# Output layer begun inside the last chunk of the last graph layer, with its own PSUM banks and a fixed TensorE order

## The chip, the cores and the metric

The kernel runs on one core of one Trainium2 chip. Its engines have queues of their own: TensorE (PE, with weight loads listed as PEld), VectorE (DVE), ScalarE (ACT), GpSimd (POOL) and SyncE (SP), which issues most DMAs. The metric is the device time of one execution in microseconds (us); the time before is the median of four runs, 2605.83 us (2600.69 to 2610.18). The profile shows one execution.

## The reference, cut to what matters

The network has four layers on a graph of N = 2708 nodes with 256 features; each layer adds a graph part and a feed-forward part to x. The change touches the graph parts of layers 2 and 3 (one function builds both) and the feed-forward part of layer 3, which is the last thing computed:

```python
def _L3_gnn_ref(h, adj, W, a):
    Wh = h @ W
    f1 = Wh @ a1
    f2 = Wh @ a2
    e = leaky_relu(f1[:, None] + f2[None, :], negative_slope=0.2)
    e = where(adj > 0, e, NEG_INF)
    return elu(softmax(e, axis=1) @ Wh)

def _L3_ffn_ref(x, weight, bias):
    return einsum('bsi,oi->bso', x, weight) + bias

x = x + _L3_gnn_ref(_layernorm(x), adj, L3_gnn_W, L3_gnn_a)
x = x + _L3_ffn_ref(_layernorm(x)[None], L3_ffn_weight, L3_ffn_bias)[0]
```

All matrices are float32.

## The kernel before

The nodes lie in 22 tiles of 128 rows (NT = 22; the last, LAST = 21, has 20 rows). X holds all features in SBUF for the whole program.

**The graph layer.** `gat_single` (L1301) is called with the key g2 for layer 2 and g3 for layer 3. After a head that builds V (features times a factor, and a column of the factor itself), `big_p` and `ratio`, the node columns are worked off in four chunks: three of six tiles (768 columns) and one of three tiles (384 columns, tiles 18 to 20). Per chunk there are 22 steps j (L1448). In a step, `gat_pairs` lets ScalarE make e from big_p (L731) and VectorE multiply it with the mask (L732); e has three buffers. TensorE then adds e's part times V[j] to one accumulator per tile (L1463). An accumulator is 128x257 float32 in a PSUM bank of its own; the pool has eight banks, so that of a new chunk's accumulators some lie in banks that the chunk before doesn't use. The 20 columns of tile 21 are computed at the last chunk's start by `tail_sums` (L81): 22 narrow matmuls (L87) into four quarters of a bank, a copy ts to SBUF on ScalarE (L89), and a matmul with `quarter` that adds the four quarters into another bank (L91).

At a chunk's end each tile is divided by its last column (VectorE's reciprocal rd, L1469). Layer 3 has an ELU behind this: ScalarE reads the accumulator into h with the scale rd (L1477), VectorE takes min(h, 0) into g (L1479), ScalarE the exponential of g (L1480), VectorE max(h, 0) - 1 (L1481), adds g and h (L1482) and adds that to X (L1483).

**The output layer.** `linear_ffn` (L2380) comes after the graph layer. It loads weight and bias by GpSimd's queue. `ln_stats` (L112) takes mean and variance in groups of four tiles by bn_stats and bn_aggr on VectorE (L160, L161), then Sqrt on ScalarE (L163) and a reciprocal on VectorE (L167). Then each tile t is normalised into f on VectorE (`normed`, L124), transposed in two halves on TensorE (L132), copied into ft on ScalarE (L2396), multiplied with the weight on TensorE (two matmuls, L139). GpSimd adds the bias to X (L2397), VectorE adds product and X into o (L2401, three buffers), and SP's queue writes o to HBM (L2402).

**What sets the order.** A framework schedules each engine's instructions by priorities and estimated times, so that instructions of the output layer that depend only on finished tiles can be put between those of the graph layer on the same engine. `tc.issue_after` holds an instruction behind a named one. Waits between engines are put in by the framework from tiles and pools; a pool that is closed gives its memory to the next one opened, which then waits for the readers of what lay there. `Stats.newton` (L169) computes the inverse square root on VectorE in twelve small operations without ScalarE; it exists before and is used in the graph layer's head.

Of the kernel before, what the change touches and what calls it, by code (L numbers as in the profile page):

```python
# [8 lines left out]
F32 = mybir.dt.float32  # L9
# [7 lines left out]
P = 128  # L17
# [18 lines left out]
def rows(t):  # L36
    return min(P, N - t * P)


def span(t):  # L40
    return slice(t * P, t * P + rows(t))
# [7 lines left out]
def tiles_of(start, length):  # L49
    return range(start // P, (start + length + P - 1) // P)  # L50


class Net:
# [27 lines left out]
    def tail_sums(self, pool, work, et, V):  # L81

        nc = self.nc
        ps = pool.tile([P, D + 1], F32, name="acc")
        for j in range(NT):
            g = j % 4 * 32
            nc.tensor.matmul(ps[g : g + 32], et[:, j, :], V[:, j, :], start=j < 4, stop=j >= NT - 4)  # L87
        ts = work.tile([P, D + 1], F32, name="ts", bufs=1)
        nc.scalar.copy(ts, ps)  # L89
        ps = pool.tile([P, D + 1], F32, name="acc")  # L90
        nc.tensor.matmul(ps[: rows(LAST)], self.quarter[:, : rows(LAST)], ts, start=True, stop=True)  # L91
        return ps

    def value(self, v, name):
        t = self.const.tile([P, 1], F32, name=name)
# [78 lines left out]
def cosine_gnn(net, ctx, kept, x_in):  # L174
# [7 lines left out]
    with ExitStack() as ctx:  # L182
# [101 lines left out]
        for n, (i0, iw) in enumerate(chunks(512)):  # L284
            its = tiles_of(i0, iw)
            adj_rows = {i: load_rows_of(i) for i in its}
            if n + 2 < len(chunks(512)):
                columns(*chunks(512)[n + 2])
            whole = [i for i in its if i < LAST]
            acc = [pacc.tile([P, D + 1], F32, name=f"acc{k}", tag=f"acc{k}") for k in range(len(whole))]  # L290
            for j in range(NT):
                r = rows(j)
                ps = psc.tile([P, 512], F32, name="score")
                nc.tensor.matmul(ps[:r, :iw], QK[:, 0, span(j)], QK[:, 1, i0 : i0 + iw], start=True, stop=True)  # L294
                e = work.tile([P, 512], F32, name="e")
                exp = nc.scalar.activation(e[:r, :iw], ps[:r, :iw], AF.Exp)  # L296

                if j % 4 == 1 and 0 <= j // 4 - 1 < len(its):
                    i = its[j // 4 - 1]
                    with tc.issue_after(exp.ins):  # L300
                        degree(i, adj_rows[i])
                w = len(whole) * P
                nc.vector.tensor_tensor(e[:r, :w], e[:r, :w], net.mask[:r, j, i0 : i0 + w], ALU.mult)  # L303
                if w < iw:
                    nc.vector.tensor_tensor(et[:r, j, : iw - w], e[:r, w:iw], net.mask[:r, j, i0 + w :], ALU.mult)
                for k in range(len(whole)):
                    ended = nc.tensor.matmul(  # L307
                        acc[k], e[:r, k * P : (k + 1) * P], F[:r, j, :], start=j == 0, stop=j == NT - 1
                    )
            if len(whole) < len(its):  # L310
                with tc.issue_after(ended.ins):
                    acc.append(net.tail_sums(ptail, work, et, F))
            nc.vector.tensor_scalar(
                deg[:, its[0] : its[-1] + 1], total[:, its[0] : its[-1] + 1], 0.0, None, ALU.is_gt
            )
            for k, i in enumerate(its):
                r = rows(i)
                g = work.tile([P, D + 1], F32, name="g", bufs=4)
                (nc.scalar.copy if k % 2 else nc.vector.tensor_copy)(g[:r], acc[k][:r])
                s = work.tile([P, 2], F32, name="s")  # L320
                nc.vector.tensor_copy(den[:r, i : i + 1], g[:r, D : D + 1])
                nc.vector.tensor_scalar(s[:r, 0:1], g[:r, D : D + 1], 1e-30, None, ALU.max)
                nc.vector.reciprocal(s[:r, 0:1], s[:r, 0:1])
                nc.vector.scalar_tensor_tensor(s[:r, 0:1], s[:r, 0:1], 0.5, deg[:r, i : i + 1], ALU.mult, ALU.mult)
                nc.vector.tensor_scalar(s[:r, 1:2], deg[:r, i : i + 1], -0.5, 1.0, ALU.mult, ALU.add)
                nc.vector.scalar_tensor_tensor(X[:r, i, :], g[:r, :D], s[:r, 0:1], X[:r, i, :], ALU.mult, ALU.add)
                nc.vector.scalar_tensor_tensor(X[:r, i, :], F[:r, i, :D], s[:r, 1:2], X[:r, i, :], ALU.mult, ALU.add)
# [970 lines left out]
            nc.vector.tensor_scalar(self.grow, self.grow, 1.0 - SLOPE, None, ALU.mult)  # L1298


def gat_single(net, key, head, feed, elu):  # L1301

# [4 lines left out]
    with ExitStack() as ctx:  # L1309
# [118 lines left out]
            nc.vector.tensor_copy(V[one_row, LAST, :D], ps[one_row])  # L1428
            nc.vector.memset(V[one_row, LAST, D:], float(N))
        work = ctx.enter_context(tc.tile_pool(name=f"{key}work", bufs=3))  # L1430
        pacc = ctx.enter_context(tc.tile_pool(name=f"{key}acc", bufs=8, space=PSUM))
        whole = LAST * P
        nc.gpsimd.memset(et, 0.0)
        ev = et[:, :, : N - whole]
# [7 lines left out]
        for i0 in range(0, whole, W):  # L1442
            iw = min(W, whole - i0)
            its = tiles_of(i0, iw)
            acc = [pacc.tile([P, D + 1], F32, name="acc") for _ in its]
            if i0 + iw == whole:
                acc.append(net.tail_sums(pacc, work, et, V))
            for j in range(NT):  # L1448
                e = work.tile([P, W], F32, name="e")
                masked = gat_pairs(net, e, j, i0, iw, big_p, ratio[:, j : j + 1])  # L1450
                if i0 == 0 and j == 3:
                    net.looped = masked
                if bias is not None and i0 == 0 and j == 3:

                    late = small.tile([P, D], F32, name="late", bufs=1)
                    with tc.issue_after(masked.ins):
                        nc.vector.tensor_copy(late, bias)
                    for t in range(NT):
                        r = rows(t)
                        nc.gpsimd.tensor_tensor(X[:r, t, :], X[:r, t, :], late[:r], ALU.add)  # L1460
                for k, i in enumerate(its):
                    ri = rows(i)
                    nc.tensor.matmul(  # L1463
                        acc[k][:ri], e[:, k * P : k * P + ri], V[:, j, :], start=j == 0, stop=j == NT - 1
                    )
            for k, i in enumerate([*its, LAST][: len(acc)]):
                r = rows(i)
                rd = small.tile([P, 1], F32, name="rd")
# [12 lines left out]
                nc.vector.tensor_scalar(h[:r], h[:r], 0.0, -1.0, ALU.max, ALU.add)  # L1481
                nc.vector.tensor_tensor(g[:r], g[:r], h[:r], ALU.add)  # L1482
                nc.vector.tensor_tensor(X[:r, i, :], X[:r, i, :], g[:r], ALU.add)  # L1483


def decoder_ffn(net, ctx):
# [874 lines left out]
def biased_gnn(net, head, route):  # L2361
    def results(ctx):
        return route.combine(ctx.enter_context(net.tc.tile_pool(name="g2y", bufs=1)))

    gat_single(net, "g2", head, results, False)


def elu_gnn(net, kept, head, route):
    def results(ctx):
        rest = route.combine(ctx.enter_context(net.tc.tile_pool(name="g3y", bufs=1)))  # L2370
        first = next(rest)
        with net.tc.issue_after(route.read.ins):
            reload_graph(net, kept)
        yield first
        yield from rest

    gat_single(net, "g3", head, results, True)


def linear_ffn(net, out):  # L2380

    nc, tc, a, X = net.nc, net.tc, net.a, net.X
    with ExitStack() as ctx:
        big = ctx.enter_context(tc.tile_pool(name="f3big", bufs=1))
        work = ctx.enter_context(tc.tile_pool(name="f3work", bufs=3))
        psum = ctx.enter_context(tc.tile_pool(name="f3p", bufs=3, space=PSUM))
        w = net.load_weight(big, a["f3_wT"], "w")
        b = net.load_rows(big, a["f3_b"], D, "b")
        ln = net.ln_stats()
        for t in range(NT):  # L2390
            r = rows(t)
            f = work.tile([P, D], F32, name="f")
            net.normed(f, t, ln)
            ps = net.transposed(psum, f, r)
            ft = work.tile([P, 2, P], F32, name="ft")
            nc.scalar.copy(ft[:, :, :r], ps[:, :, :r])  # L2396
            nc.gpsimd.tensor_tensor(X[:r, t, :], X[:r, t, :], b[:r], ALU.add)  # L2397
            po = psum.tile([P, D], F32, name="po")
            net.matmul_k(po[:r], ft[:, :, :r], w)
            o = work.tile([P, D], F32, name="o")  # L2400
            nc.vector.tensor_tensor(o[:r], po[:r], X[:r, t, :], ALU.add)  # L2401
            nc.sync.dma_start(out[span(t), :], o[:r])  # L2402


@with_exitstack
def net_kernel(ctx, tc, a, out):
# [14 lines left out]
    with ExitStack() as mixture:  # L2421
        head, route = decoder_ffn(net, mixture)
        with ExitStack() as graph:
            net.mask = graph.enter_context(tc.tile_pool(name="mask2", bufs=1)).tile([P, NT, N], U8, name="mask2")
            elu_gnn(net, kept, head, route)
    linear_ffn(net, out)


def clear_dispatch(net, pool):
# [121 lines left out]
```

## Time and profile before

| | |
|---|---|
| median of four runs | 2605.83 us (2600.69 to 2610.18) |
| profiled execution, its own time | 2614.9 us |
| its span in the profile | 2613.0 us |
| TensorE busy in the span | 2433.3 us, 93% |
| VectorE, ScalarE, GpSimd busy | 1477.2, 1052.0, 334.4 us |
| mean granted TensorE clock | 0.963 |
| steps of chunk three of layer 3 end, last chunk's tail sums start | 2544.29 us |
| last chunk's first step starts on TensorE | 2548.16 us |
| transposes of the output layer start | 2580.18 us |
| last addition of the output layer starts | 2610.01 us |

Times in a timeline row are: start from the beginning of the span, busy time, engine, line, operation, what is written and read, shape, count; in brackets how long the engine idled before and which instruction ended that. A float32 matmul appears as two records, a transpose as one. Rows of equal instructions are merged, so a row's busy time can cover several. In a table by stretches the columns are the stretch, its length, busy time and count of PE, PEld, DVE, ACT and POOL, the granted TensorE clock (1.00 is full), the DMA share and GB/s.

### The profile page before, as it was taken

What the parts mean: (1) busy time and instruction counts of PE and PEld (TensorE: products, weight loads), DVE (VectorE), ACT (ScalarE), POOL (GpSimd) and SP (SyncE); (2) the same over time, 40 slices, a digit from 0 to 9 for tenths busy, and PEclk for the clock granted to TensorE, in tenths of its full rate; (3) what the DMA queues carried; (4) which work ended last, traced back from release to release, by engine and by line L of the source; (5) the groups of instructions that cost most, each with busy time, mean ns of one, the idle gap of its engine ahead of it and who ended that gap; (6) DMA issues with size and microseconds to landing.
All of it is one profiled execution on the core that took longest, in us unless ns stands there. A gap on an engine that the chain in (4) does not pass through costs nothing. (4 is left out here: it accounts for less than half of the span.)

```text
span 2613.0 us, 32662 instructions
## 1 busy us (share of the span) xinstructions
PE 2433.3 (93%) x11708; PEld 1582.1 (61%) x11708; DVE 1477.2 (57%) x3288; ACT 1052.0 (40%) x1692; POOL 334.4 (13%) x476
## 2 busy tenths in 40 slices
PE   6899998999999998979799989999989999969998
PEld 4666765686333334568578854444457777747886
DVE  7753437745888876333544457788742222264556
ACT  3444453214877772321434333344422222234454
POOL 1000003100000001144130011222221111110002
PEclk9999999979999999989899999999989999979999
DMA  8899611000000003764220010000241111050001
GB/s 288 284 289 314 204 55 64 1 6 1 1 1 1 1 1 91 180 182 144 88 66 1 1 31 17 19 17 17 107 147 34 33 33 33 19 205 7 1 1 43
DMA packets 106859, 197.58 MB, mean 76 GB/s; under 512 B 8862, under 2 KB 63752, under 8 KB 103860
## 3 DMA queue, kind: packets, MB, share of 16 engines
q1 hardware_dynamic: 88010, 146.82, 18.4%
q0 software_dynamic: 14880, 43.76, 5.2%
q10 hardware_dynamic: 3806, 4.85, 0.6%
q8 instruction: 99, 1.62, 0.3%
q14 instruction: 64, 0.52, 0.1%
HBM read 135.69 MB, written 59.71 MB: 75 GB/s over the span
## 5 line engine op out<-in xcount | busy, mean ns | idle before, releaser
L732 DVE SCALAR_TENSOR_TENSOR e<-e,mask 128x768 f32<-128x768 f32 (+3 forms) x352 | 417.3, 1216 | 244.1 <-ACT e L731 241.8
L731 ACT ACTIVATE e<-big_p,minus_one,ratio 128x768 f32<-128x768 f32 (+3 forms) x352 | 418.6, 1226 | 282.5 <-PE acc L1463 195.3
L1463 PE MATMUL acc<-V,e 128*128 128x257 f32 x1848 | 403.6, 381 | 5.7 <-DVE e L732 5.6
L1463 PEld LDWEIGHTS acc<-V,e 128*128 128x128 f32 x1848 | 351.6, 191 | 57.9 <-issue 7.0
L2226 PE MATMUL h<-w,ft 128*128 (+1 forms) x752 | 234.6, 454 | 0.5 <-ACT ft L2208 0.5
L307 PE MATMUL acc<-F,e 128*128 128x257 f32 (+1 forms) x924 | 212.5, 383 | 4.1 <-DVE e L303 3.8
L928 PE MATMUL acc<-e,V 128*64 128x512 f32 (+1 forms) x1056 | 208.0, 546 | 1.3 <-DVE e L732 1.3
L307 PEld LDWEIGHTS acc<-F,e 128*128 128x128 f32 (+1 forms) x924 | 171.6, 189 | 56.9 <-DVE e L303 29.6
L2243 DVE TENSOR_TENSOR hh<-hh,h 128x682 f32<-128x682 f32 x47 | 40.7, 865 | 243.7 <-PE h L2226 243.7
L2226 PEld LDWEIGHTS h<-w,ft 128*128 128x128 f32 x752 | 135.9, 191 | 56.5 <-issue 1.8
L928 PEld LDWEIGHTS acc<-e,V 128*64 128x64 f32 x1056 | 73.4, 137 | 150.3 <-issue 144.9
L2014 ACT ACTIVATE e<-sc 128x1024 f32<-128x1024 f32 (+4 forms) x131 | 107.7, 863 | 139.6 <-PE sc L2005 110.3
L303 DVE TENSOR_TENSOR e<-e,mask 128x512 f32<-128x512 f32 (+2 forms) x132 | 80.3, 620 | 140.5 <-ACT e L296 138.8
L2036 DVE TENSOR_TENSOR sum<-sum,e 128x1024 f32<-128x1024 f32 (+4 forms) x131 | 137.0, 1046 | 23.6 <-ACT e L2014 10.1
L296 ACT ACTIVATE e<-score 128x512 f32<-128x512 f32 (+2 forms) x132 | 69.4, 544 | 171.0 <-PE score L294 145.8
L2258 PE MATMUL po<-w,ht 114*128 (+1 forms) x564 | 131.5, 383 | 0.9 <-DVE ht L2251 0.9
L2005 PE MATMUL sc<-qt,kt 64*128 64x512 f32 (+5 forms) x568 | 122.4, 549 | 1.1 <-ACT sum L2014 0.9
L2258 PEld LDWEIGHTS po<-w,ht 114*128 114x128 f32 x564 | 107.6, 191 | 23.0 <-DVE ht L2251 7.8
L939 PE MATMUL den<-e,low 128*3 128x512 f32 (+1 forms) x1056 | 117.7, 542 | 0.0
L294 PE MATMUL score<-QK 128*128 128x512 f32 (+2 forms) x264 | 112.1, 554 | 3.4 <-ACT e L296 3.0
L2030 PE MATMUL po<-e,V 128*64 128x512 f32 (+5 forms) x524 | 109.4, 535 | 1.9 <-DVE e L2020 1.9
L2252 ACT COPY ht<-pt 114x256 f32<-114x256 f32 x47 | 17.5, 372 | 200.7 <-DVE ht L2251 200.7
(647 smaller groups left out, 3392.5 us busy)
## 6 DMA issues: line engine op xcount, KB each, us to landing
row<-in_adj SPq DMA_DIRECT2D x21, 1354.0 KB
raw<-in_adjT SPq DMA_DIRECT2D x35, 768.0 KB
hs<-zero SPq DMA_DIRECT2D x8, 2838.0 KB
hidden<-hr SPq DMA_DIRECT2D x32, 256.0 KB
wd<-in_f_wd SPq DMA_DIRECT2D x8, 1024.0 KB
kept<-mask SPq DMA_DIRECT2D x21, 338.5 KB
mask<-kept SPq DMA_DIRECT2D x21, 338.5 KB
w<-in_d_w1T SPq DMA_DIRECT2D x8, 682.0 KB
```

Source lines behind the costliest of these rows:

```text
L294: nc.tensor.matmul(ps[:r, :iw], QK[:, 0, span(j)], QK[:, 1, i0 : i0 + iw], start=True, stop=True)
L307: ended = nc.tensor.matmul(acc[k], e[:r, k * P : (k + 1) * P], F[:r, j, :], start=j == 0, stop=j == NT - 1)
L731: nc.scalar.activation(v, big_p[:, i], AF.Relu, bias=net.minus_one, scale=ratio)
L732: return nc.vector.scalar_tensor_tensor(v, v, 1.0, net.mask[:, j, i], ALU.add, ALU.mult)
L928: nc.tensor.matmul(acc[n][half, :iw], V[:, j, h, :], e[n][:, k, :iw], start=j == 0, stop=j == NT - 1)
L939: nc.tensor.matmul(den[g : g + Q, :iw], low[:, j, h, Q - 1 - q : 2 * Q - 1 - q], e[n][:, k, :iw], start=False, stop=j == NT - 1 and q == Q ...
L1463: nc.tensor.matmul(acc[k][:ri], e[:, k * P : k * P + ri], V[:, j, :], start=j == 0, stop=j == NT - 1)
L2005: nc.tensor.matmul(by_pairs(ps[:r, g], m, iw)[:, :, o:], kt[b, span(j)], qt[b, :, o:iw], start=True, stop=True)
L2030: nc.tensor.matmul(by_pairs(outs[n, p][b], m, iw)[:, :, o:], V[:r, j, g, :], by_pairs(e[:r, g], m, iw)[:, :, o:], start=j == 0, stop=j == ...
L2036: nc.vector.tensor_tensor(total, total, by_heads(e[:r], m, iw)[:, :, :, o:], ALU.add)
L2226: last = nc.tensor.matmul(halves[s, n][:, q, :HALF], fts[s][:, c, :], weights.w13[n][:, es[s], c, q * HALF : (q + 1) * HALF], start=c == 0 ...
L2258: last = nc.tensor.matmul(po, ht[:KP, k, :], w2[:KP, es[s], k, :], start=k == 0, stop=k == KC - 1)
```

## The change

`linear_ffn` becomes a class `Linear`, whose parts are called from `gat_single`.

- `open`, after the graph layer's head: loads weight and bias, and opens the SBUF pools, ahead of chunk one.
- `begin`, ahead of the last chunk of layer 3: the pool of eight PSUM banks is closed; a pool f3p with three banks (one for transposes, two for products) and a pool of five banks for the last chunk's accumulators are opened. Mean and variance of tiles 0 to 11 are taken, with `newton` in place of Sqrt. From here on TensorE's instructions stand in the order in which they are written (`manual_schedule`).
- `step`, in each step j of the last chunk: from j = 2 one tile is normalised per step, behind that step's mask product, and GpSimd adds the bias to X for it; steps 7 to 12 take mean and variance of tiles 12 to 17, step 13 their Newton root. Tiles 0 and 1 are transposed in steps 18 and 20. 18 buffers hold f.
- `finish`, after the last ELU: for each tile t the transposes of tile t + 2, then the product of t, the addition and the DMA. The statistics of tiles 18 to 21 are taken at t = 4, with Sqrt.
- `tail_sums` is split: the 22 narrow matmuls and the copy come ahead of the last chunk's steps, and allocate their bank first; the matmul with `quarter` is called after step 2. This holds for layers 2 and 3. Layer 0 calls both at once as before.

```diff
         ts = work.tile([P, D + 1], F32, name="ts", bufs=1)
         nc.scalar.copy(ts, ps)
-        ps = pool.tile([P, D + 1], F32, name="acc")
-        nc.tensor.matmul(ps[: rows(LAST)], self.quarter[:, : rows(LAST)], ts, start=True, stop=True)
-        return ps
+
+        def added():
+            ps = pool.tile([P, D + 1], F32, name="acc")
+            nc.tensor.matmul(ps[: rows(LAST)], self.quarter[:, : rows(LAST)], ts, start=True, stop=True)
+            return ps
+
+        return added
...
-def gat_single(net, key, head, feed, elu):
+def gat_single(net, key, head, feed, tail=None):
...
-        pacc = ctx.enter_context(tc.tile_pool(name=f"{key}acc", bufs=8, space=PSUM))
+        if tail:
+            tail.open(ctx)
+        elu, room = tail is not None, ctx.enter_context(ExitStack())
+        pacc = room.enter_context(tc.tile_pool(name=f"{key}acc", bufs=8, space=PSUM))
...
+            ending = elu and i0 + iw == whole
+            if ending:
+                room.close()
+                tail.begin(room, its[0])
+                pacc = room.enter_context(tc.tile_pool(name=f"{key}end", bufs=5, space=PSUM))
+                ctx.enter_context(tc.manual_schedule(engines={mybir.EngineType.PE}))
+            if i0 + iw == whole:
+                added = net.tail_sums(pacc, work, et, V)
             acc = [pacc.tile([P, D + 1], F32, name="acc") for _ in its]
-            if i0 + iw == whole:
-                acc.append(net.tail_sums(pacc, work, et, V))
...
+                if j == 2 and i0 + iw == whole:
+                    acc.append(added())
+                if ending:
+                    tail.step(j, masked)
...
+            if ending:
+                tail.finish()
...
-def linear_ffn(net, out):
...
+class Linear:
...
+    def open(self, ctx):
+
+        net, tc = self.net, self.net.tc
         big = ctx.enter_context(tc.tile_pool(name="f3big", bufs=1))
+        self.work = ctx.enter_context(tc.tile_pool(name="f3work", bufs=3))
+        self.w = net.load_weight(big, net.a["f3_wT"], "w")
+        self.b = net.load_rows(big, net.a["f3_b"], D, "b")
+        self.ln = Stats(net)
+        self.fs, self.fts = {}, {}
+
+    def begin(self, ctx, open_from):
+
+        self.psum = ctx.enter_context(self.net.tc.tile_pool(name="f3p", bufs=1, space=PSUM))
+        self.early = open_from
+        self.ready = 0
+        self.known(0, self.early - 6)
+
+    def known(self, t0, t1):
+        self.ln.sums(t0, t1, root=False)
+        self.ln.newton(self.work, t0, t1)
+        self.have = t1
+
+    def norm(self, t):
+        r, X = rows(t), self.net.X
+        self.fs[t] = self.work.tile([P, D], F32, name="f", bufs=self.early)
+        self.net.normed(self.fs[t], t, (self.ln.mean, self.ln.rstd))
+        self.net.nc.gpsimd.tensor_tensor(X[:r, t, :], X[:r, t, :], self.b[:r], ALU.add)
+
+    def step(self, j, masked):
+
+        with self.net.tc.issue_after(masked.ins):
+            if 6 < j < 13:
+                self.ln.sums(self.early + j - 13, self.early + j - 12, root=False)
+            if j == 13:
+                self.ln.newton(self.work, self.early - 6, self.early)
+                self.have = self.early
+            if j > 1 and self.ready < self.have:
+                self.norm(self.ready)
+                self.ready += 1
+        if j in (NT - 4, NT - 2):
+            self.turned(len(self.fts))
+
+    def turned(self, t):
+        net, r = self.net, rows(t)
+        ps = net.transposed(self.psum, self.fs.pop(t), r)
+        ft = self.fts[t] = self.work.tile([P, 2, P], F32, name="ft", bufs=4)
+        net.nc.scalar.copy(ft[:, :, :r], ps[:, :, :r])
+
+    def result(self, t):
+        net, nc, r = self.net, self.net.nc, rows(t)
+        po = self.psum.tile([P, D], F32, name="po", bufs=2)
+        net.matmul_k(po[:r], self.fts.pop(t)[:, :, :r], self.w)
+        o = self.work.tile([P, D], F32, name="o")
+        nc.vector.tensor_tensor(o[:r], po[:r], net.X[:r, t, :], ALU.add)
+        nc.sync.dma_start(self.out[span(t), :], o[:r])
+
+    def finish(self):
+
         for t in range(NT):
...
+            if t == 4:
+                self.ln.sums(self.early, NT)
+                self.ln.roots(self.early, NT)
+            if t + 2 < NT:
+                if t + 2 not in self.fs:
+                    self.norm(t + 2)
+                self.turned(t + 2)
+            self.result(t)
```

## The prediction

> **What bounds the kernel now.** I read the page first, then TensorE's timeline around the last chunk, then VectorE's and ScalarE's there, then the output layer, and last two older places whose rows price things that the stretch itself doesn't show.
>
> ```profile
> span 2613.0 us, 32662 instructions
> PE 2433.3 (93%) x11708; PEld 1582.1 (61%) x11708; DVE 1477.2 (57%) x3288; ACT 1052.0 (40%) x1692; POOL 334.4 (13%) x476
> ```
>
> TensorE is busy 93% of the span: where it waits, time is lost, elsewhere hardly. The change works in the last 70 us. TensorE there:
>
> ```profile
> 2544.29 2.79 PE L87 MATMUL acc<-V,et 128*32 128x257 f32 x44
> 2547.62 0.61 PE L91 MATMUL acc<-ts,quarter 128*20 128x257 f32 x2 [0.53 <-ACT ts L89]
> 2548.16 28.90 PE L1463 MATMUL acc<-V,e 128*128 128x257 f32 x132
> ...
> 2580.18 0.84 PE L132 MATMUL tp<-ident,f 128*128 128x128 f32 x6 [3.13 <-ACT h L1477]
> ...
> 2586.03 0.41 PE L132 MATMUL tp<-ident,f 128*128 128x128 f32 x2 [2.00 <-DVE f L124]
> ...
> 2589.85 2.86 PE L139 MATMUL po<-w,ft 128*128 128x256 f32 x12
> ...
> 2593.44 2.86 PE L139 MATMUL po<-w,ft 128*128 128x256 f32 x12
> ```
>
> The tail sums start right behind chunk three (2544.29); the last chunk is 22 steps of 28.90/22 = 1.31 us and ends at 2577.05. Then the output layer: waits of 3.13 and 2.00 us, from 2587 three tiles per 3.59 us, 0.35 of it a wait for ScalarE's copy, so 1.08 us of work per tile. The last addition ends at 2610.42. 33.4 us lie between, for about 23.4 us of matmuls: 22 products at 0.86 and 20 transposed tiles at 0.22.
>
> ScalarE and VectorE behind chunk three:
>
> ```profile
> 2542.93 1.28 ACT L1480 ACT_TABLE_LOAD   x1
> ...
> 2550.47 0.47 ACT L1477 ACTIVATE h<-acc,rd 128x256 f32<-128x256 f32 x1
> ```
>
> The second row reads the sixth accumulator. It ends at 2550.94, and nobody on TensorE waits for it now: the last chunk's banks are others.
>
> **The change part by part.** The sum is made against the profiled execution (2614.9 us, span 2613.0), which lies 9.1 above the median of the four runs, 2605.83; I apply the difference to the median.
>
> *Own banks: +4.3.* Old and new pool share eight banks, and the old one is closed first. In the built program of the changed kernel the first tail matmul (L87) waits for ScalarE's h of the sixth accumulator, and the nine matmuls behind it wait for nothing more; before, L87 waited for a bank of chunk two, and the first three matmuls each for one accumulator. So the whole ELU of chunk three is now ahead of TensorE, and behind that wait stand all of its instructions. When does that h end? Before, from VectorE's first g+h (L1482, 2544.67) to its end (2550.94) it took 6.27 us, mostly VectorE's queue. The first exponential no longer waits for its table load (1.28), because the statistics no longer use Sqrt in between: the first g+h starts near 2543.7, the h ends at 2550.0. Bounds: 2550.94 (no gain) and 2549.66 (all of 1.28). TensorE idles 5.7 us. But the chunk now follows the 22 tail matmuls directly: 2.42 us after 2550.0 instead of 3.87 after 2544.29, so 2552.4 against 2548.16.
>
> *Moved into the chunk: +0.95.* The quarter matmul stands behind step 2 (0.45), where ts is long there, and two tiles' transposes stand in steps 18 and 20 (0.82 for six: 0.5). TensorE bounds those steps.
>
> *In the second graph layer: -0.9.* There the quarter matmul moves too, without new pools; the wait for ts ahead of it (0.9 between the rows' starts) is covered by three steps.
>
> *Normalisation in the steps: +2.4.* Per step VectorE gets f (0.36) beside the mask product e (0.56), GpSimd an addition (0.72); steps 7 to 12 also a bn_stats and bn_aggr (0.5), and 13 to 15 a chain of twelve small operations, 0.2 each. By VectorE alone this fits into 1.31 us. But GpSimd and VectorE get in each other's way:
>
> ```profile
> 1331.38 1.50 DVE L732 SCALAR_TENSOR_TENSOR e<-e,mask 128x768 f32<-128x768 f32 x1 [0.59 <-ACT e L731]
> ...
> 1346.99 0.96 DVE L732 SCALAR_TENSOR_TENSOR e<-e,mask 128x768 f32<-128x768 f32 x1 [1.63 <-ACT e L731]
> ```
>
> ```profile
> 1329.94 8.37 POOL L1460 TENSOR_TENSOR X<-X,late 128x256 f32<-128x256 f32 x8
> ```
>
> The same e takes 0.96 alone and up to 1.50 beside the same kind of addition, which itself takes 1.05 instead of 0.72: they take turns. In the old output layer four f beside four additions took 2.99 us, 0.75 per pair. So a step needs 0.56 + 0.75 and something for the third turn, 1.44 I take, against 1.31: 18 steps x 0.13 = 2.3; the chain adds 12 x 0.2 = 2.4; e's three buffers give back about 2.3. Bounds: 0 (all fits), and all in series, 0.56 + 0.41 + 0.72 = 1.69, 18 x 0.38 = 6.8, with the chain and less 1.3 of slack 8.0. I take 2.4, near the pair that was measured. f lies beside TensorE's steps; without that cover it costs 18 x 0.36 = 6.5.
>
> *Fixed order afterwards: -5.7.* The 23.4 us of matmuls follow the chunk. Four waits are left, each read off the queues. (a) The third transposes have one bank and wait for the copy of tile 2, which stands on ScalarE behind four h and two exponentials: 1.0. (b) Product 2 waits for o(0), which stands on VectorE behind the ELU of four tiles: 1.3. (c) The one Sqrt left loads its table (1.28) between two copies: 0.5. (d) Four late f and their additions stand ahead of o(6): 0.8. With 0.7 for the last product's drain and addition: 27.7 against 33.4. Output transfers follow every 1.08 instead of 1.20 us on SP's queue; three o buffers give each 3.2 us. Bounds: no waits, -9.3; waits twice as long, -2.1.
>
> *Clock: +2.1.* A gap costs the granted clock:
>
> ```profile
> 1524.14:1530.04 5.90, 0.07 (x2) 0.04 (x1) 5.90 (x44) 0.59 (x2) 1.19 (x3) 0.79 0.65 161
> 1530.04:1534.30 4.26, 4.26 (x19) 3.67 (x20) 3.48 (x22) 1.17 (x2) 0.00 (x0) 0.50 0.31 110
> ```
>
> After an idle 5.83 us TensorE ran 4.26 us at half clock: 2.1 lost. That gap is nearest to the 5.7 of the new stall. Bounds: 0, and the whole gap's length at half, 2.9. A shorter gap was also enough (2.24 us ahead of 1888.18, then 3.40 us at 0.50), while the 3.13 us ahead of 2580.18 were not.
>
> The Trainium skill, "TensorE: Matmul & The Clock Gate", section "Why this matters for your kernels", asks for no TensorE gap above about 3 us, as one idle window puts the clock at half; this speaks against the new stall. By its window of 3.4 us the estimate is 1.7 lost and the sum 2608.6; the rows differ on the gap, since 2.24 us sufficed and 3.13 didn't.
>
> **Sum:** 4.3 + 0.95 - 0.9 + 2.4 - 5.7 + 2.1 = +3.2 us. The profiled span becomes 2616.2, the median **2609.0 us** (+0.12%). What this kernel's measurement can tell from no change is about 0.3%, 7.8 us: below 2598.0 is faster, above 2613.6 slower.
>
> **Rivals.**
> 1. *The stall isn't there* (the wait is met early, the chunk's ELU being quicker): the chunk starts 1.4 earlier than before, no clock loss, the steps fit: -1.4 + 0.95 - 0.9 - 5.7 = -7.1, **2598.7**. For it: before, TensorE had no gap at this place. Against: the wait in the built program names the sixth h. 0.12, half of it faster.
> 2. *VectorE and GpSimd bound the last chunk* (slower): all in series, 8.0 instead of 2.4, **2614.6**. It decides once a step's e, f and addition exceed 1.31 us by 0.35. For it: the 1.50 row. Against: the 0.75 pair. 0.18.
> 3. *The layer is started early but doesn't end earlier*: the waits (a) to (d) are twice as long, **2612.6**. For it: one transposing bank, two product banks, and o behind the ELU. Against: ScalarE and VectorE have idle time at 2578 now. 0.15, a quarter of it slower.
>
> The forecast has 0.55. Faster: 0.06 + 0.01 for the rest of the low side = 0.07; slower: 0.18 + 0.04 = 0.22; within 0.3%: 0.71. The bounds together reach from -5.4 (3.9 + 0.95 - 0.9 + 0 - 9.3 + 0; rival 1 lies below it) to +14 (5.2 + 0.95 - 0.9 + 8.0 - 2.1 + 2.9); ends that need every bound at once are left out: 2601 to 2616.
>
> **What shows it.** A TensorE gap of 5.4 to 6.7 us ahead of the last L87, with the sixth h as its end, and 3 to 4 us of half clock behind it; chunk steps of 1.3 to 1.45 us with e waiting beside GpSimd; gaps of about 1 us ahead of the third transposes and the third product; then 1.08 us per tile. Wrong would be: no gap ahead of L87, steps above 1.6 us, or an output layer still paced at 1.2 us.

## The result and the profile after

The median after is 2611.37 us (51 runs, 2600.15 to 2619.88) against 2606.89 us before (78 runs, 2597.9 to 2619.3; the four shown above are among them). The medians differ by 4.5 us. The ratio of the runs is 1.0014, with a 95% interval of 1.0007 to 1.0021: 3.6 us slower, between 1.8 and 5.5. The forecast was 3.2 us.

The profiled execution after is no longer than the one before (own time 2614.49 us against 2614.9):

```profile
span 2612.6 us, 32637 instructions
PE 2426.9 (93%) x11708; PEld 1574.8 (60%) x11708; DVE 1482.2 (57%) x3307; ACT 1045.6 (40%) x1681; POOL 337.1 (13%) x476
```

Two executions can't be compared by their spans here: runs of one kernel differ by about 20 us, and this one was already 6.7 us ahead at the first chunk of the second graph layer (key g2), before the first changed instruction. So I compare the stretch in which the programs differ: from the first matmul of chunk three to the end of the last output addition, read off single starts in the traces. It takes 123.46 us before and 127.72 after, 4.3 longer; the second graph layer gives 0.36 back, which leaves 3.9.

TensorE after, in the same view as before (start, busy time, instruction, idle time ahead of it and what ended it):

```profile
2529.66 10.35 PE L1476 MATMUL acc<-V,e 128*128 128x257 f32 x47
2545.79 4.87 PE L87 MATMUL acc<-V,et 128*32 128x257 f32 x44 [5.79 <-ACT h L1494]
2550.59 4.17 PE L1476 MATMUL acc<-V,e 128*128 128x257 f32 x18
...
2573.31 4.17 PE L1476 MATMUL acc<-V,e 128*128 128x257 f32 x18 [0.47 <-DVE e L736]
...
2583.77 0.44 PE L136 MATMUL tp<-ident,f 128*128 128x128 f32 x2 [0.86 <-ACT ft L2451]
...
2586.32 1.13 PE L143 MATMUL po<-w,ft 128*128 128x256 f32 x4 [1.03 <-DVE o L2458]
...
2591.14 0.44 PE L136 MATMUL tp<-ident,f 128*128 128x128 f32 x2 [0.44 <-ACT ft L2451]
...
2601.98 1.13 PE L143 MATMUL po<-w,ft 128*128 128x256 f32 x4 [0.20 <-DVE o L2458]
```

Chunk three ends at 2540.01, and TensorE stands until 2545.79. The 22 tail matmuls behind it take 4.87 us, where they took 2.79. Behind the last chunk (its last matmul starts at 2581.44) only short waits are left. The stall ends with this row of ScalarE, the h of the sixth accumulator:

```profile
2545.22 0.47 ACT L1494 ACTIVATE h<-acc,rd 128x256 f32<-128x256 f32 x1 [1.30 <-DVE rd L1486]
```

The stretches of the same trace (length, then busy time of PE, PEld, DVE, ACT and POOL, granted clock, DMA) say why the tail matmuls are slow:

```profile
2545.79:2550.59 4.80, 4.80 (x44) 2.37 (x44) 1.81 (x4) 0.42 (x1) 0.51 (x1) 0.56 0.02 3
2550.59:2581.66 31.07, 30.60 (x141) 25.23 (x140) 24.30 (x62) 14.91 (x24) 15.62 (x17) 1.00 0.00 1
```

The clock is 0.56 over the tail matmuls and 1.00 from the first step on.

### The profile page after: what moved, and what is told of

The parts are those of the page before. It is cut to its first block, busy times and chain, and to the rows that moved or that the text cites. A ratio compares the mean times of both kernels' runs of the same rounds, so it can differ in the third digit from the quotient of the medians.

```text
span 2612.6 us, 32637 instructions
## 1 busy us (share of the span) xinstructions
PE 2426.9 (93%) x11708; PEld 1574.8 (60%) x11708; DVE 1482.2 (57%) x3307; ACT 1045.6 (40%) x1681; POOL 337.1 (13%) x476
## 4 chain that ended last, share of the span: by engine, by line
PE 34%; issue 7%; DVE 5%; DMA 3%; POOL 1%; ACT 1%; DVEq 0%; POOLq 0%; ACTq 0%; SPq 0%
PE h L2245 7%; PE acc L1476 7%; PE po L2277 4%; PE sc L2024 3%; PE po L2049 3%; PE pj L1995 2%; PE pv L143 2%; DMA dys<-y,to 2%; DVE sum L2055 1%; PE pt L2269 1%; DVE yt L2068 1%; POOL X L1473 1%; PE s1p L1378 1%; PE wy L143 1%; PE po L143 1%
```

## The experiments

All kernels at a glance, in us, each from its one profiled execution. "Wait and sums" runs from the last matmul of chunk three to the first step of the last chunk, "chunk" from there to that chunk's last matmul, "behind" from there to the end of the last addition. "From last" is the sum of these three, which the expectations use; "from first" adds chunk three. The ratio is to runs of the kernel before that were taken beside each kernel.

| kernel | chunk three | wait and sums | chunk | behind | from last | from first | ratio to before, 95% |
|---|---|---|---|---|---|---|---|
| before | 57.02 | 4.18 | 28.52 | 33.75 | 66.44 | 123.46 | |
| after | 57.35 | 10.97 | 30.85 | 28.56 | 70.37 | 127.72 | 1.0014 (1.0007 to 1.0021) |
| one pool | 57.36 | 3.03 | 31.22 | 24.60 | 58.86 | 116.22 | 0.9953 (0.9933 to 0.9973) |
| one pool, again | 57.36 | 3.03 | 31.30 | 24.61 | 58.94 | 116.30 | 0.9978 (0.9960 to 0.9996) |
| sums first | 57.36 | 6.13 | 32.45 | 28.08 | 66.66 | 124.01 | 0.9974 (0.9957 to 0.9991) |
| stall filled | 57.36 | 8.84 | 30.86 | 28.09 | 67.80 | 125.15 | 1.0019 (1.0006 to 1.0032) |
| no bias | 57.36 | 11.46 | 29.84 | 27.58 | 68.88 | 126.24 | 0.9998 (0.9975 to 1.0021) |
| free normalisation | 59.78 | 10.46 | 31.10 | 28.08 | 69.63 | 129.42 | 1.0022 (1.0004 to 1.0040) |
| three f buffers | 57.36 | 11.47 | 29.69 | 29.09 | 70.24 | 127.60 | 1.0026 (1.0006 to 1.0045) |
| free order | 57.36 | 11.34 | 30.77 | 28.11 | 70.22 | 127.58 | 1.0016 (0.9995 to 1.0036) |
| spread | 61.48 | 3.03 | 29.69 | 24.61 | 57.33 | 118.81 | 0.9983 (0.9961 to 1.0005) |
| spread, again | 61.48 | 3.03 | 29.69 | 24.61 | 57.33 | 118.81 | 0.9990 (0.9980 to 1.0000) |
| lead only | 57.02 | 4.17 | 28.52 | 30.97 | 63.66 | 120.68 | 0.9998 (0.9985 to 1.0010) |
| shared lead | 57.02 | 4.18 | 28.52 | 30.39 | 63.09 | 120.10 | 0.9999 (0.9987 to 1.0012) |

The stretch repeats to 0.1 us in the two pairs of equal kernels, the medians don't: they carry the scatter of the other 2480 us. Both pairs are kernels without the stall; in the five in which TensorE idles through it, the tail matmuls alone took 4.28 to 5.29 us, so there the stretch can differ by 1 us for no edit. The stretch's difference from before, less the 0.36 us for kernels made from the changed one, lies in the interval of the ratio in eleven of the thirteen comparisons. It lies outside for "sums first" (+0.2 us by the stretch, the interval ends at -2.3) and just outside for "stall filled" (+1.3, the interval begins at +1.6). Both leave the mechanisms alone: I judge sizes of a few us by the stretch, and whether a kernel is faster by the ratio.

**One pool.** The theory was that closing the pool makes the stall.

```diff
-                room.close()
-                tail.begin(room, its[0])
-                pacc = room.enter_context(tc.tile_pool(name=f"{key}end", bufs=5, space=PSUM))
+                tail.begin(pacc, its[0])
...
-        ps = net.transposed(self.psum, self.fs.pop(t), r)
+        ps = self.psum.tile([P, D + 1], F32, name="acc")[:, :D].rearrange("p (c q) -> p c q", c=2)
...
-        po = self.psum.tile([P, D], F32, name="po", bufs=2)
+        po = self.psum.tile([P, D + 1], F32, name="acc")[:, :D]
```

> The pool of eight banks stays open; the last chunk's accumulators, the transposes and the products take their banks from it in turn, so each waits for the last reader of one bank only. Theory (the wait for the closed pool makes the stall, and the stall the half clock): no gap of 5.8 us ahead of the tail sums, 22 of them in 2.8 us instead of 4.9, last chunk's first step about 8 us earlier against the end of chunk three; the waits of 0.86 and 1.03 us behind the last chunk, for one transposing bank and two product banks, shrink too; about 1 us comes back because the rest of the ELU now lies beside the first steps. Sum -8 -1.9 +1: about 2602.5 us. Rival A (it is the ELU of chunk three that TensorE has to wait for, whatever the pool): the gap stays, 2609 to 2612 us. Rival B (the ELU, moved into the steps, pushes the mask products back there as much as the stall cost): no gap ahead of the tail sums, but steps two to six above 2 us each, 2608 to 2611 us.

```profile
2527.27 2.79 PE L87 MATMUL acc<-V,et 128*32 128x257 f32 x44
2530.00 4.17 PE L1474 MATMUL acc<-V,e 128*128 128x257 f32 x18
...
2561.65 1.03 PE L143 MATMUL acc<-w,ft 128*128 128x256 f32 x4
```

In this TensorE timeline the tail matmuls have no bracket: no wait, 2.79 us, and the first step 2.7 us behind them. The stretch is 11.5 us shorter than the changed kernel's and 7.2 shorter than before. Both rivals fall: the ELU still runs, beside the steps, and costs two steps 0.1 to 0.2 us each. Behind the chunk every tile takes 1.08 us from the first on, 4.0 us less than after; I had expected 1.9.

> The kernel with one pool of eight banks once more, for a second measurement beside the kernel before: the stretch from the last matmul of chunk three to the last addition is 58.9 us against 66.4 before, so 7 to 8 us less; the 12 us of its first measurement then hold 4 to 5 us from elsewhere, where the program is the same. If the change of the pool is worth 12 us somewhere, this run shows 12 again.

It came out at 6.6 us less by the medians and 5.7 by the ratio, interval 1.0 to 10.4; the stretch has 7.2. So the 12 us of the first run held about 5 us of scatter.

**Sums first.** The 22 tail matmuls go ahead of the closing, into the old pool.

```diff
+            if i0 + iw == whole:
+                added = net.tail_sums(pacc, work, et, V)
             if ending:
                 room.close()
...
-            if i0 + iw == whole:
-                added = net.tail_sums(pacc, work, et, V)
```

> As the changed kernel, but the 22 narrow matmuls of the tail sums are written ahead of the closing of the pool and take a bank of the old one, so TensorE has 2.7 us of work in the stall. Theory: they start right behind chunk three, the gap behind them is 5.8 - 2.7 = 3.1 us, and the last chunk's first step comes 4.8 us earlier if the clock stays full (2606.6 us), 3.1 us earlier if this gap still costs a window of half clock (2608.3 us). Rival (the stall is not the wait for the closed pool): the tail sums wait as before, 2611.4 us.

TensorE's timeline, then the stretch behind the wait:

```profile
2529.18 2.79 PE L87 MATMUL acc<-V,et 128*32 128x257 f32 x44
2534.99 5.86 PE L1476 MATMUL acc<-V,e 128*128 128x257 f32 x18 [3.02 <-ACT h L1494]
```

```profile
2534.99:2538.50 3.51, 3.51 (x10) 2.83 (x11) 2.30 (x5) 1.12 (x2) 0.56 (x1) 0.60 0.00 0
```

The wait moves behind the tail matmuls and is 3.02 us, as worked out. It still costs clock: 0.60, and three steps take 5.86 instead of 4.17, 1.7 us. From the last matmul of chunk three to the last addition it is 3.7 us less than after, 3.1 were expected for this case. The rival falls.

**Stall filled.** This takes the clock apart from the wait.

```diff
             if ending:
+                for _ in range(2):
+                    ps = pacc.tile([P, D + 1], F32, name="acc")
+                    for k in range(NT):
+                        g = k % 4 * 32
+                        nc.tensor.matmul(ps[g : g + 32], et[:, k, :], V[:, k, :], start=k < 4, stop=k >= NT - 4)
                 room.close()
```

> As the changed kernel, with 44 more narrow matmuls of the tail-sums kind into two free banks of the old pool, ahead of its closing; nothing reads them. They take 5.4 us, so TensorE works through the stall, which itself stays. Theory (the idle stall costs granted clock): the real tail sums take 2.7 us instead of 4.3 to 5.3, the stretch from the last matmul of chunk three to the last addition falls from 70.4 to about 68.3 us; the wait for the sixth h stays and ends where it did. Rival (the tail sums are slow there for another reason): 70.4.

```profile
2535.36 5.39 PE L1458 MATMUL acc<-V,et 128*32 128x257 f32 x88
2541.17 2.79 PE L87 MATMUL acc<-V,et 128*32 128x257 f32 x44 [0.42 <-ACT h L1499]
```

The real tail matmuls still wait for the sixth h, 6.1 us behind chunk three, but take 2.79 us again. The same wait without idleness costs 2.1 us less in this row (4.80 to 2.72 between starts). So wait and clock are two separate terms. The stretch fell to 67.8; 68.3 was expected.

**No bias.** The additions of the bias on GpSimd are left out.

```diff
-        self.net.nc.gpsimd.tensor_tensor(X[:r, t, :], X[:r, t, :], self.b[:r], ALU.add)
```

> As the changed kernel, but GpSimd's addition of the bias to X is left out for all tiles, so the output lacks the bias. Theory of the forecast (VectorE and GpSimd take turns in each step, 2.4 us in the chunk, and four late additions stand ahead of an output addition): the chunk behind its first step shrinks by 2.4 us and the layer behind it by 0.2 to 0.8, 2608.2 to 2608.8 us. Theory by the changed kernel's trace (only the twelve small operations of the root, and what piles up behind them, delay the steps, 1.2 us in all, and part of that is their turns with an addition): -0.5 to -1.5 us, 2609.9 to 2610.9. Rival (VectorE's own queue makes the delay): no change, 2611.4.

In TensorE's timeline the sixteen steps behind the quarter matmul, j = 3 to 18, now form one row without a wait (steps are counted from 0 here, as j in the kernel; the expectation of "spread" counts them from 1):

```profile
2550.97 21.09 PE L1476 MATMUL acc<-V,e 128*128 128x257 f32 x96
```

That is 21.09 less 0.17 of overlap, over 16 steps, 1.31 us each. After had the same sixteen steps with 1.2 us of delay, all of it in steps 13 to 16 (1.38, 1.54, 2.04, 1.40 us); the nine steps 4 to 12, each with its f and its addition, took 1.30. So my forecast of 1.44 us in each step falls, and so does the rival that VectorE's queue alone makes the delay: the addition is needed. Here is what it does, in VectorE's timeline of the changed kernel:

```profile
2567.16 0.69 DVE L343 TENSOR_SCALAR nrx<-mv 128x6 f32<-128x6 f32 x1
...
2568.28 0.71 DVE L347 TENSOR_SCALAR rstd<-nrh 128x6 int32<-128x6 int32 x1
...
2572.18 1.08 DVE L736 SCALAR_TENSOR_TENSOR e<-e,mask 128x384 f32<-128x384 f32 x1
...
2601.50 0.76 DVE L2458 TENSOR_TENSOR o<-po,X 128x256 f32<-128x256 f32 x2 [1.59 <-DMA out<-o]
```

Two of the root's operations, on six numbers per partition, take 0.7 us beside additions that start at 2566.76 and 2568.25 on GpSimd. In the kernel without the additions the same two take 0.17:

```profile
2562.90 0.17 DVE L343 TENSOR_SCALAR nrx<-mv 128x6 f32<-128x6 f32 x1
...
2563.50 0.17 DVE L347 TENSOR_SCALAR rstd<-nrh 128x6 int32<-128x6 int32 x1
```

The mask product then takes 1.08 instead of 0.56. In the steps ahead of the root, each with a pair and statistics, VectorE's mask products followed every 1.27 us, just inside TensorE's 1.30. From the last mask product ahead of the root to the fourth behind it, it is 7.22 us in the changed kernel and 5.21 without the additions. TensorE loses 1.2 us of these 2.0, since some e were made ahead. (The last row of the changed kernel's fence belongs to the layer behind, below.)

**Free normalisation.** The steps call it for tiles 0 and 1 only, and the framework places the rest.

```diff
-            if j > 1 and self.ready < self.have:
-                self.norm(self.ready)
-                self.ready += 1
+        if j in (NT - 6, NT - 5):
+            self.norm(self.ready)
+            self.ready += 1
```

> As the changed kernel, but the steps of the last chunk no longer call the normalisation, except for tiles 0 and 1; it is called after the chunk and the framework places it where it finds room: by the built program 12 of the 18 fall into chunk three and six behind the root in the last chunk. Statistics and roots stay in the steps. Theory: chunk three has 1.6 us to spare on VectorE per step and hides its share, the last chunk's steps lose their delay of 1.2 us, the layer behind it stays 28.3 us: 2610.2 us. Rival (what is moved into chunk three delays chunk three, since its mask products take 1.40 to 1.50 us beside an addition instead of 0.96): 2612 to 2614 us.

The rival holds. Chunk three takes 2.4 us more, in one step of 4.92 us instead of 2.60, and the last chunk keeps its delay, since the framework puts three f between two mask products behind the root. "From last" misses chunk three's loss; this is why the table also has "from first".

**Spread.** On one pool, tiles 0 to 11 ahead of the last chunk, 12 to 17 in steps 15 to 20.

```diff
         self.known(0, self.early - 6)
+        for t in range(self.have):
+            self.norm(t)
+        self.ready = self.have
...
-            if j > 1 and self.ready < self.have:
+            if j > 14 and self.ready < self.have:
```

> As the kernel with one pool of eight banks, but tiles 0 to 11 are normalised ahead of the last chunk (the framework puts them into chunk three) and tiles 12 to 17 in steps 15 to 20, behind the root of step 13, so that no normalisation stands beside the small operations of the root or the ELU of chunk three. By the trace of the one-pool kernel its chunk loses 1.7 us (steps 5, 6 and 14 to 17) against 1.30 us a step. Theory (root, normalisation and the turns with GpSimd's additions piled up there): these steps fall to 1.30 to 1.40, the stretch from the last matmul of chunk three to the last addition goes from 58.9 to 57.5 us. Rival (the root alone, twelve operations between two mask products, makes the delay): 58.5 to 58.9. Rival (VectorE and GpSimd in chunk three delay chunk three): its steps above 2.60 us.

TensorE's timeline in chunk three and in the last chunk:

```profile
2498.96 35.77 PE L1474 MATMUL acc<-V,e 128*128 128x257 f32 x156 [2.17 <-DVE e L736]
...
2542.02 21.09 PE L1474 MATMUL acc<-V,e 128*128 128x257 f32 x96
```

The second row is the theory's: no delay left, and 57.33 us from the last matmul of chunk three against 57.5 expected. The first is the second rival's: TensorE waits 2.17 us for a mask product in chunk three. VectorE and GpSimd there, of the same kernel:

```profile
2493.43 4.07 DVE L128 TENSOR_SCALAR f<-X,mv,rstd 128x256 f32<-128x256 f32 x6
2497.43 1.48 DVE L736 SCALAR_TENSOR_TENSOR e<-e,mask 128x768 f32<-128x768 f32 x1
```

```profile
2494.33 5.16 POOL L2432 TENSOR_TENSOR X<-X,b 128x256 f32<-128x256 f32 x6 [0.23 <-DVE f L128]
```

The framework put six f between two mask products. In turns with six additions they take 4.07 us, and the mask product 1.48 instead of 0.96; a step of 2.60 us can't hold that. With the half clock that followed the gap, chunk three takes 4.1 us more than in the one-pool kernel, and "spread" ends 2.6 us behind it. One f per step of chunk three, written so, would be the version to make; it wasn't tried.

> The kernel with one pool and spread normalisation once more, beside the kernel before: the stretch was 57.3 us against 66.4, TensorE-bound from end to end, so 9 us less; its first measurement showed 2.2 us less with an interval of 10. Expected is 5 to 12 us less.

It measured 2.6 us less by the ratio, interval 0 to 5.2. That is less than the 9 us of the expectation, which didn't count chunk three's loss; with it the stretch says 4.7 (5.0 with the second layer's part).

**Three f buffers** (in addition to the edit of "free normalisation", `bufs=self.early` is left off f) and **free order** (the line with `manual_schedule` is left out) ask what shortens the layer behind the chunk.

```diff
-        self.fs[t] = self.work.tile([P, D], F32, name="f", bufs=self.early)
+        self.fs[t] = self.work.tile([P, D], F32, name="f")
```

> As the changed kernel (own banks, fixed order), but only tiles 0 and 1 are normalised in the last chunk and f has three buffers, as before; the rest is normalised behind the chunk. Statistics and roots stay in the steps. Theory (the early normalisation is what lets the output layer run at TensorE's 1.08 us per tile; f 0.40, the addition on GpSimd in turns with it, 0.75 together, and o 0.42 are 1.17 us): about 1.2 us per tile behind the chunk, that stretch goes from 28.6 to 31 us, the last chunk loses its 1.2 us of delay; from the last matmul of chunk three to the last addition 71.2 to 72.0 us against 70.4. Rival (TensorE's order and the early start alone bring the gain): the stretch behind the chunk stays at 28.6 us, 69.2 in all.

```diff
-                ctx.enter_context(tc.manual_schedule(engines={mybir.EngineType.PE}))
```

> As the changed kernel, but without the fixed order for TensorE: the framework orders the instructions behind the start of the last chunk. By the built program only the first eight tiles behind the chunk differ (five transposes ahead of the third product). Theory (the gain behind the chunk comes from the early normalisation, not from the written order): from the last matmul of chunk three to the last addition 70 to 71 us against 70.4. Rival (the fixed order itself is worth the 5 us): 73 us or more.

Three buffers cost 1.0 us behind the chunk against 28.08, nearly all of it one wait in TensorE's timeline:

```profile
2574.88 0.41 PE L136 MATMUL tp<-ident,f 128*128 128x128 f32 x2 [1.12 <-DVE f L128]
```

From there on it also runs at 1.08 us per tile. My expectation of 1.2 falls: f, addition and o need not follow one another, and fit into 1.08. As the last chunk has no delay without the f (29.69 against 30.85), the early normalisation gains nothing in sum. The free order takes 28.11: the written order is worth nothing either. Both times I had the wrong cause for the 5 us.

**Lead only** makes a third try, on the kernel before: the transposes two tiles ahead of the product.

```diff
+        turned(0)
+        turned(1)
         for t in range(NT):
             r = rows(t)
-            f = work.tile([P, D], F32, name="f")
...
+            if t + 2 < NT:
+                turned(t + 2)
+            ft = fts.pop(t)
```

> The kernel before, with one edit: the output layer transposes two tiles ahead of the product, as the changed kernel does. Pools, statistics and normalisation are as before. The kernel with three f buffers showed that the early normalisation isn't what shortens the output layer, and the one without a fixed order that the order isn't. Theory (the lead of two tiles takes the waits for ScalarE's copy, 0.35 us per three tiles and 0.29 at the end, about 2.4 in all; the 3.13 and 2.00 us at the layer's start stay): the stretch from the last matmul of chunk three to the last addition 64 us against 66.4. Rival (VectorE's f, GpSimd's addition and o, 1.17 us per tile, pace the layer): 66 or more.

```profile
2569.62 0.85 PE L132 MATMUL tp<-ident,f 128*128 128x128 f32 x6 [3.12 <-ACT h L1477]
2570.62 4.54 PE L139 MATMUL po<-w,ft 128*128 128x256 f32 x12
...
2575.70 0.41 PE L132 MATMUL tp<-ident,f 128*128 128x128 f32 x2 [0.32 <-DVE rstd L167]
```

The 3.12 us ahead of the layer stay, and the steady pace is 1.08 us per tile. The later wait of 2.00 becomes 0.32, but the lead didn't do that: the three products ahead of it take 4.54 us, where the same row before (at 2581.17) took 2.86, because here the gap of 3.12 us was followed by a lower granted clock (the second-last number):

```profile
2570.62:2575.00 4.38, 4.38 (x13) 3.50 (x14) 4.13 (x17) 2.93 (x7) 0.32 (x1) 0.61 0.09 32
```

The 1.68 us that the products lose are the 1.68 that the wait lost. The layer takes 2.8 us less than before, 2.4 expected, mostly by the pace (1.08 instead of 1.20 us per tile). This is about half of what the change gained there. The whole kernel's ratio can't show it: 0.9998, between 3.9 us faster and 2.6 slower.

**Shared lead** gives this kernel the graph layer's pool as well.

```diff
-        psum = ctx.enter_context(tc.tile_pool(name="f3p", bufs=3, space=PSUM))
...
+        if elu:
+            linear_ffn(net, net.out, pacc)
```

> As the kernel before with the lead of two tiles, and the output layer takes its banks from the graph layer's pool, which stays open; nothing is normalised in the steps beyond what the three f buffers allow. Theory (the kernel before had the wait for a closed pool already, 3.13 us behind the last chunk; the change only moved it ahead of the chunk and made it longer): this wait goes, the layer's start then waits for f only, the stretch is 61 to 62.5 us against 64 with the lead alone. Rival (the 3.13 us are the ELU itself or the transposes' data): 64.

```profile
2574.22 0.82 PE L2399 MATMUL acc<-ident,f 128*128 128x128 f32 x6
2577.72 1.13 PE L139 MATMUL acc<-w,ft 128*128 128x256 f32 x4 [2.68 <-ACT ft L2401]
...
2584.31 0.41 PE L2399 MATMUL acc<-ident,f 128*128 128x128 f32 x2 [2.22 <-DVE f L124]
```

The theory was half right. The wait for the closed pool goes: the transposes follow the chunk at once. But the first product then waits 2.68 us for ScalarE's copy, which stands behind the ELU, and f is late by 2.22. Only 0.6 us is gained by the stretch. That speaks for the change's two transposes inside the last chunk, with their copies ahead of the ELU, as what makes the start quick; no run had this edit alone.

## Why the prediction was right, point by point

The direction, the size and the largest terms held. The terms as measured by the stretch, with 3.9 us in sum against 3.2 (the ratio has 3.6):

- **Own banks, +4.3: right, 4.7.** The gap was 5.79 us against 5.7, ended by the sixth h as said. The filled kernel has 8.84 us at full clock where before has 4.18. Of the 0.4 that the term was short, 0.3 is the tail matmuls, which take 2.72 us from their start to the chunk's first step, not 2.42.
- **Clock, +2.1: right, 2.1.** The tail matmuls took 4.80 us between starts instead of 2.72. In the four other kernels with this stall they took 4.28 to 5.29, so one execution pays 1.6 to 2.6 us there; that this one paid what the nearest gap had is luck.
- **Moved into the chunk, +0.95: right.** The quarter matmul's step took 1.93 instead of 1.30 us, the one behind it 1.40, and the two steps with transposes 1.52: 1.17 in sum.
- **The second graph layer, -0.9: too large, 0.36.** The quarter matmul started 3.27 us behind the first tail matmul, and 2.72 of that are the tail matmuls, so the wait was 0.55. The quarter matmul costs 0.2 more between two steps (0.73) than it did ahead of the first (0.54). Before and after, TensorE's timelines there:

```profile
1491.50 2.79 PE L87 MATMUL acc<-V,et 128*32 128x257 f32 x44
1494.77 0.61 PE L91 MATMUL acc<-ts,quarter 128*20 128x257 f32 x2 [0.47 <-ACT ts L89]
1495.31 28.90 PE L1463 MATMUL acc<-V,e 128*128 128x257 f32 x132
```

```profile
1484.82 2.79 PE L87 MATMUL acc<-V,et 128*32 128x257 f32 x44
1487.54 4.17 PE L1476 MATMUL acc<-V,e 128*128 128x257 f32 x18
1491.64 0.61 PE L93 MATMUL acc<-ts,quarter 128*20 128x257 f32 x2
```

- **Normalisation in the steps, +2.4: too large, 1.2, and placed wrongly.** This is the step that failed. Turns between VectorE and GpSimd exist, but a step has room for one pair; only the root's twelve operations together with the additions run over. From the 0.75 us per pair I had concluded 1.44 us in every step; it was 1.30 in nine of them. One step of 2.04 us lies above the 1.6 that I had named as a sign of being wrong.
- **Fixed order afterwards, -5.7: the size right, 5.2, the name wrong.** The four waits came where they were listed: 0.86 (1.0 forecast), 1.03 (1.3), 0.44 (0.5), 0.18 (0.8). A fifth of 0.20 wasn't listed: an output DMA took 3.61 us where I had given it 3.2, and o's three buffers made VectorE wait 1.59 us. It is the execution's own; the comparable kernels show 28.1 us without it. But the written order is worth 0.0 and the early normalisation at most 1.0: 2.8 us are the lead of two tiles. The rest, 1.9 of the 5.7 that a kernel without this DMA wait gains, I put down to the two tiles transposed ahead of the ELU; that is argued, not shown.
- **Not foreseen, +0.3:** the first step of chunk three takes 2.94 us instead of 2.60 in all kernels made from the changed one. There the third tile's weight load waits 0.47 us for an h of chunk two (`ACT h L1494`), in front of which ScalarE makes an e. At the start of chunk two it does so in every kernel, the one before too, and that step takes 2.94 as well. Before, a table load of 1.28 us at chunk three's start held up the first exponential, and that h came ahead of the e. So the missing Sqrt is the likely cause; no run has it alone.

The terms are off by 0.4, 0.2, 0.5, 0.5 and 0.3 us to one side and by 1.2 to the other. That the sum came out 0.7 from the forecast is partly luck.

Of the rivals, the first (no stall) and the third (tail waits doubled) didn't come. The second was near in mechanism, but one step with a pair fits; it came true where the framework piles up six pairs, in "spread".

## What to carry to other kernels

A pool that is closed between two stages makes the next stage's first instruction wait for the last reader of every buffer, so close it where the engine that would wait has other work, or take both stages' buffers from one pool in turn: here this was 11.5 us by the stretch between the changed kernel and its one-pool form, which beats the kernel before in two comparisons. A stage's gain should be traced to one edit before it is credited: a lead of two tiles in the old code had half of it, by the stretch, for a few lines. When work is hidden under another stage, one piece per step cost nothing in nine steps here; left to the scheduler, it was bunched and cost 2.4 and 4.1 us in chunk three, where as a tail it costs about 1.0.

## What the runs showed of the hardware

- Short gaps can cost granted clock, and the length of the gap alone doesn't decide. Ahead of the first chunk of layer 3 all fourteen traces have the same gap of 2.82 or 2.83 us. The step behind it took 2.68 us in four of them, at a clock of 1.00. It took 4.15 to 4.36 in eight, and 5.27 with 0.46 more in the next step in two: nothing, 1.5 to 1.7, or 3.0 us for one gap. The gap of 3.12 or 3.13 us ahead of the output layer was followed by a clock of 1.00 before (2577.05 to 2584.00, around the gap) and by 0.61 in "lead only". 5.8 us cost 1.6 to 2.6 us depending on the execution, and 3.02 us cost 1.7. The 2.17 us in chunk three of "spread" was followed by a step of 4.17 us instead of 2.60, with a granted clock of 0.64 over 4.24 us; behind a gap of 2.16 us in "free normalisation" the next step took 2.70.
- The Trainium skill, "TensorE: Matmul & The Clock Gate", section "Part 1: The HAM clock gate (the "warmup" mystery)", has the clock follow an activity window of 3.41 us that runs freely. If so, a gap's price depends on where it falls in the windows, which would fit the uneven prices above; no run here sees the windows themselves. The page's rule against gaps above about 3 us (section "Why this matters for your kernels") doesn't fit the 2.17, nor the 2.83.
- An addition of 128x256 on GpSimd can hold up even a tiny VectorE operation: 0.17 us became 0.7 for six numbers per partition.
